# A Chebyshev graph layer's first sweep: the last row's end in two halves of 256 columns, and the other tiles' sums added one tile ahead

## The chip, the core and the metric

The kernel runs on one core of a Trainium2 chip. It uses TensorE (PE, matmuls and transposes into PSUM), VectorE (DVE), ScalarE (ACT), GpSimd (POOL) and the DMA queues of SyncE (SP), ACT and POOL. The metric is the device time of one execution in microseconds (us); the time of a kernel is the median of its runs. The profiles are single executions taken by the hardware profiler, and their times count from the first instruction ("span").

## The reference

Four graph layers run one after the other over the same 4096 x 4096 matrix, each with a residual and a layer norm. The change touches layer 0 and the beginning of layer 3.

```python
# layer 0: x is 4096 x 64, L is adj (4096 x 4096), weight is 4 x 64 x 64
terms = [x, L @ x]
for _ in range(2, K):                       # K = 4
    terms.append(2.0 * (L @ terms[-1]) - terms[-2])
out = jnp.einsum('kni,kio->no', jnp.stack(terms, axis=0), weight)
x = _layernorm(x + out)
...
# layer 3: log map between all pairs of rows, weighted by adj / deg
log_ij = _logmap(x[:, None, :], x[None, :, :], c)
agg = jnp.einsum('ij,ijc->ic', w, log_ij)
x = _layernorm(x + _expmap(origin, agg @ weight + bias, c))
```

## The kernel before

**Layout.** The 4096 rows are 32 blocks of 128; four blocks are a group (8 groups, NG). A tile is 512 rows of group g by 512 columns of chunk c. `cheb_n[:, block, n, :]` holds three terms of 64 features per block: term 0 is ready from the start, term 1 of a group is added to when that group's first sums are done, term 2 after that.

**The first sweep** (the loop `for g in range(NG)`, L643) goes through the rows g = 0 to 7, and in each row through c = 7 down to 0. One pass of the inner loop loads a raw tile (L121, SP queue), turns it block by block on PE (L657), copies it out on ACT (`at`, L664), stores it (L686, POOL queue), and then reduces the raw tile twice on DVE: row sums (`dpart`, L688) and minimum (`lows`, L690). The products of a tile are one tile late: `tile_before`, called behind the next tile's transposes. Tiles with c >= g multiply term 0 only, 64 columns at a time in the two halves of the bank `h_ps` (`halves`, L559); at c = g these sums go to SBUF as `t_h`. Tiles with c < g multiply terms 0 and 1 at once, 128 columns into the bank `w_ps` (`both`, L566). So the lower half of `w_ps` holds more of the first sums, the upper half a part of the second sums.

**The end of a row** is `after_first` (L598), called when the products of c = 0 have been issued. It adds the lower half of `w_ps` to `t_h` (L604, DVE), copies the upper half to `t_w` (L605, ACT), and returns four steps. `first` turns `t_h` on PE and adds it into term 1 (`twice_into`: L580 transposes and two additions for groups above 4, L585 products with `pair`, which add the two halves of a block, and one addition for the others; L588 is the addition). `on_diagonal` multiplies the diagonal tile with the new term 1 into the bank `d_ps` and adds `t_w`, giving `t_d` (L614). `second` does with `t_d` for term 2 what `first` did for term 1, and `taken_off` subtracts term 1 from `nat_a` on POOL (L622). For rows 0 to 6 the steps are taken one per pass of the next row's loop. For row 7 nothing follows, and they run behind the loop, L693 to L695.

**The second sweep** (L745) starts then. Its first product (`pass2`, L566, bank `h_ps`) is that of group 6 with chunk 7, and needs terms 1 and 2 of group 7. Its tiles are loaded on the SP queue (L712) into the buffers that held raw tiles, and each is compared with 0 on DVE (`four`/`mask`, L754). SP also waits for a flag, `no_negative` (L706), which is worked out from `lows` by a one-column product (`low_ps`, L705).

**What sets the order.** Instructions in `in_order(...)` keep their place among each other on their engine; the others may be moved ahead by the scheduler that builds the program, as far as their operands allow. Every engine then works off its own list in order and waits on semaphores.

**Layer 3** is a loop of steps `n`, two for each 512 x 512 tile of pairs, with pieces of several steps interleaved: PE products (`product(n + 2)`, L1494; `opposite`, L1513; `gather`, L1555 and L1567; `turn`, L1539), ACT functions (L1503, L1718, L1719, L1745, L1754) and DVE work (L1521, L1728, L1731, L1743, L1541). At the end of every step one entry of the list `seam` is run (L1757). On entry to the loop the list holds 14 steps: for groups 0 and 1 and then for groups 2 and 3 the end of layer 2 (`ends`: sums, roots, rest, `prepare`, and one `turn_prepared` for each group, L1217 and L1218, which puts the group's features into `tr_a`, also named `tr_c`), and then `weights` and `factors`. `product(12)` and `product(13)` read group 2 in `tr_c`. At one step per `n` the turn of group 2 is run at the end of n = 10.

Of the kernel before, what the change touches and what calls it, by code (L numbers as in the profile page):

```python
# [9 lines left out]
F32 = mybir.dt.float32  # L10
# [5 lines left out]
ALU = mybir.AluOpType  # L16
# [46 lines left out]
def gnn4_kernel(  # L63
# [21 lines left out]
    nc = tc.nc  # L85
    P = 128
    N, F = x.shape
    NB = N // P
    GB = 4
    GW = GB * P  # L90
    NG = NB // GB
    CB = 4
# [49 lines left out]
    pair = const.tile([P, F], F32, name="pair")  # L142
# [25 lines left out]
    nat_a = keep.tile([P, NB, F], F32, name="nat_a")  # L168
# [36 lines left out]
    def in_order(ins):  # L205
        return tc.keep_in_program_order(ins)

    def cols(b):
        return slice(b * P, (b + 1) * P)

    def gblocks(g):
        return slice(g * GB, (g + 1) * GB)
# [312 lines left out]
    with tc.tile_pool(name="acc", bufs=1) as acc_p, tc.tile_pool(  # L525
        name="cols0", bufs=4
    ) as cols_p, tc.tile_pool(name="kept0", bufs=1) as kept_p, tc.tile_pool(name="diag0", bufs=2) as diag_p, tc.tile_pool(
        name="ps_t0", bufs=3, space=PSUM
    ) as ps_t, tc.tile_pool(name="ps_a0", bufs=1, space=PSUM) as ps_a, tc.tile_pool(
        name="ps_p0", bufs=2, space=PSUM  # L530
    ) as ps_p:

        cheb_n = acc_p.tile([P, NB, 3, F], F32, name="cheb_n")

        t_w = [acc_p.tile([P, GW], F32, name=f"t_w{q}") for q in range(2)]
# [28 lines left out]
        def both(ps, k, rhs, jb, first, last):  # L564

            in_order(nc.tensor.matmul(ps, lhsT=cheb_n[:, jb, k : k + 2, :], rhs=rhs, start=first, stop=last))  # L566

        def out_of(ps, name):
            t = acc_p.tile([P, GW], F32, name=name, tag=name if name == "t_h" else "tcol", bufs=2)
            nc.scalar.copy(t, ps)  # L570
            return t

        def new_post(w=F):
            return ps_p.tile([P, GB, w], F32, name="post", tag="post")
# [49 lines left out]
            return [first, on_diagonal, second, taken_off]  # L624


        win = ExitStack()
        win_p = win.enter_context(tc.tile_pool(name="win", bufs=1, side="right"))
        loads, weight_steps = attention_weights(win_p, ps_p)
# [6 lines left out]
        while weight_steps:  # L636
            row, c = divmod(len(aside), NCH)
# [5 lines left out]
        for g in range(NG):  # L643
            h_ps = ps_a.tile([P, GW], F32, name="h_ps")
            w_ps = ps_a.tile([P, GW], F32, name="w_ps") if g else None
            row = {}
            for c in reversed(range(NCH)):
                raw = first_raw.pop() if first_raw else load_raw(g, c)
                if g == NG - 1 and 4 <= c < g:
                    at = kept_p.tile([P, CB, GW], F32, name="at", tag="at") if c == g - 1 else before[:, c - 4]  # L650
                else:
                    at = (diag_p if c == g else cols_p).tile([P, CB, GW], F32, name="at", tag="at")
                for k in range(CB):
                    jb = c * CB + k
                    tp = ps_t.tile([P, GW], F32, name="tp", tag="tp")
                    for b in range(GB):
                        in_order(nc.tensor.transpose(tp[:, cols(b)], raw[:, b, cols(k)], ident))  # L657
                        if g * GB + b == jb:
                            scrap = sm.tile([P, P], F32, name="scrap")
                            in_order(nc.vector.scalar_tensor_tensor(  # L660
                                scrap, raw[:, b, cols(k)], 1.0, ident, ALU.mult, ALU.mult,
                                accum_out=diag[:, jb : jb + 1],
                            ))
                    nc.scalar.copy(at[:, k, :], tp)  # L664
                if steps0:
                    steps0.pop(0)()
                if tile_before:
                    tile_before()

                def tile_before(h_ps=h_ps, w_ps=w_ps, c=c, at=at, g=g, row=row):  # L670
                    for k in range(CB):
                        jb = c * CB + k
                        if c < g:
                            both(w_ps, 0, at[:, k, :], jb, c == g - 1 and k == 0, c == 0 and k == CB - 1)
                        else:
                            halves(h_ps, 0, at[:, k, :], jb, c == NCH - 1 and k < 2, c == g and k >= CB - 2)
                    if c == g:
                        row["at"] = at
                        row["t_h"] = out_of(h_ps, "t_h")
                    if c == 0:  # L680
                        steps0.extend(after_first(g, row["t_h"], w_ps, row["at"]))

                if aside:
                    for work in aside.pop(0):
                        work()
                nc.gpsimd.dma_start(adj_t[g][:, c * CB : (c + 1) * CB, :], at)  # L686

                in_order(nc.vector.tensor_reduce(dpart[:, g, c, :], raw, AX.X, ALU.add))  # L688
                n = g * NCH + c
                in_order(nc.vector.tensor_reduce(lows[:, n : n + 1], raw.rearrange("p b j -> p (b j)"), AX.X, ALU.min))  # L690
                if g == NG - 1 or (g == NG - 2 and c == g):
                    here[g, c] = at
# [52 lines left out]
        for g in reversed(range(NG - 1)):  # L745
            ps = ps_a.tile([P, GW], F32, name="pass2", tag=("h_ps", "w_ps")[g % 2])
            for c in reversed(range(g + 1, NCH)):
                at = load0(g, c)
# [16 lines left out]
        due, n = [], 0  # L765
        for m, g in enumerate(third_rows):
            ps = ps_a.tile([P, GW], F32, name="pass3", tag=("h_ps", "w_ps")[m % 2])
            row = list(reversed(range(g + 1)))
            if m == 0:
                row = row[4:] + row[1:4] + row[:1]  # L770
            for c in row:
                at = load0(g, c, None if (g, c) in here else third_pools.pop(0))
# [399 lines left out]
    for signed in (False, True):  # L1172
        with cmp.Else() if signed else tc.If(all_positive > 0) as block:
            cmp = block
            with tc.tile_pool(name="cols1", bufs=3 if not signed else 2) as cols_p, tc.tile_pool(name="sign1", bufs=1) as sg, tc.tile_pool(
                name="tail1", bufs=1
            ) as tl, tc.tile_pool(name="ps_a1", bufs=1 if signed else 2, space=PSUM) as ps_a, tc.tile_pool(
                name="ps_p1", bufs=2, space=PSUM
# [141 lines left out]
    with tc.tile_pool(name="mask2", bufs=3) as mk_p, tc.tile_pool(name="wt2", bufs=3) as wt_p, tc.tile_pool(  # L1320
        name="ps_c2", bufs=1, space=PSUM
    ) as ps_c, tc.tile_pool(name="ps_a2", bufs=1, space=PSUM) as ps_a, tc.tile_pool(
        name="ps_p2", bufs=2, space=PSUM
# [30 lines left out]
        for turn, groups in enumerate(turns_of):  # L1354
# [9 lines left out]
            for h in reversed(range(2 * NB)):  # L1364
                jb, odd = divmod(h, 2)
                c, k = divmod(jb, CB)
# [59 lines left out]
    with tc.tile_pool(name="o3", bufs=1) as op, tc.tile_pool(name="cols3", bufs=3) as cols_p, tc.tile_pool(  # L1426
# [278 lines left out]
        n = 0  # L1705
        while n < NU + 2 or turns or gathers:
            if n % 2:
                load_own((n + 1) // 2)
                load_mirrored((n - 1) // 2)
            after = gather(*gathers.pop(n)) if n in gathers else []  # L1710
            turned = [w for what in turns.pop(n, []) for w in turn(what)]
            if n < NU:
                if n % 2 == 0:
                    fs[n // 2] = fp.tile([P, CB, GW], F32, name="f3")
                w, cs = ws[n][:, :, columns(n)], columns(n)
                rts[n] = el.tile([P, HB, GW], F32, name="rt3")
                rt = rts[n][:, :, cs]
                nc.scalar.activation(w, w, AF.Ln)  # L1718
                nc.scalar.activation(rt, w, AF.Exp, scale=0.5)  # L1719
                square(n + 1)  # L1720
                opposite(n + 1)
            if n >= 2 and n - 2 < NU:
                m = n - 2
                t, h = divmod(m, 2)
                cm = columns(m)
                hs = slice(h * HB, (h + 1) * HB)
                f, at = fs[t][:, hs, cm], own[t][:, hs, cm]
                nc.vector.scalar_tensor_tensor(  # L1728
                    f, rts.pop(m)[:, :, cm], T_MAX, ws.pop(m)[:, :, cm], ALU.min, ALU.mult
                )  # L1730
                nc.vector.tensor_tensor(at, at, f, ALU.mult)  # L1731
                diagonal = tiles[t][0] == tiles[t][1]
                before = t - 1 if t and tiles[t - 1][0] != tiles[t - 1][1] else None
                gathers[n + 1] = (t, h, before)
                if diagonal and h == 0:
                    late_turns[n + 1] = (t, 0)
                if not diagonal and h == 1:
                    turns.setdefault(n + 1, []).append((t, 0))
                    turns.setdefault(n + 2, []).append((t, 1))
            for work in turned:  # L1740
                work()
            if n < NU:
                nc.vector.scalar_tensor_tensor(rt, vs[n][:, :, cs], (1.0 + V_FLOOR) * SCALE, rt, ALU.max, ALU.add)  # L1743
                product(n + 2)
                nc.scalar.activation(w, w, AF.Exp, scale=-0.5)  # L1745
            late = turn(late_turns.pop(n)) if n in late_turns else []
            for work in after:
                work()
            less_one(n + 1)
            for work in late:  # L1750
                work()
            if 0 < n <= NU:
                rt = rts[n - 1][:, :, columns(n - 1)]
                nc.scalar.activation(rt, rt, AF.Ln, scale=1.0 / SCALE)  # L1754
            if n == NU - 6:
                seam += [ahead_of_last(g) for g in seq[-2:]]
            if seam:  # L1757
                seam.pop(0)(ps_p)
            if n + 6 < NU and tiles[(n + 6) // 2][0] not in rights:
                i = tiles[(n + 6) // 2][0]  # L1760
                rights[i] = right(i)
            n += 1
# [51 lines left out]
```

## Time and profile before

| What | Value |
|---|---|
| Runs | 1411.5, 1417.04 and 1420.06 us, median 1417.04 us |
| Profiled execution, its own time | 1415.59 us |
| Its span | 1413.9 us |
| Mean granted TensorE clock | 0.976 of full speed |
| Busy: PE, DVE, ACT, POOL | 1308.5, 1052.1, 803.7, 109.8 us |
| Last product of the first sweep ends | 351.75 us |
| First product of the second sweep starts | 359.64 us |
| Layer 3's first products start | 976.5 us |

PE is busy for most of the span, but a busy share is an average over stages. For the change the stretch from 340 to 372 us and the beginning of layer 3 (976 to about 1060 us) are of interest. In the rows, L566 is line 566 of the kernel, `t_h<-w_ps,t_h` is what is written from what is read, x4 is a number of instructions, and the brackets say how long the engine had been idle and what released it. A float32 matmul shows as two passes, so four matmuls of 512 columns are x8.

### The profile page before, as it was taken

What the parts mean: (1) busy time and instruction counts of PE and PEld (TensorE: products, weight loads), DVE (VectorE), ACT (ScalarE), POOL (GpSimd) and SP (SyncE); (2) the same over time, 40 slices, a digit from 0 to 9 for tenths busy, and PEclk for the clock granted to TensorE, in tenths of its full rate; (3) what the DMA queues carried; (4) which work ended last, traced back from release to release, by engine and by line L of the source; (5) the groups of instructions that cost most, each with busy time, mean ns of one, the idle gap of its engine ahead of it and who ended that gap; (6) DMA issues with size and microseconds to landing.
All of it is one profiled execution on the core that took longest, in us unless ns stands there. A gap on an engine that the chain in (4) does not pass through costs nothing.

```text
span 1413.9 us, 18980 instructions
## 1 busy us (share of the span) xinstructions
PE 1308.5 (93%) x6766; PEld 604.3 (43%) x6766; DVE 1052.1 (74%) x2012; ACT 803.7 (57%) x1339; POOL 109.8 (8%) x191
## 2 busy tenths in 40 slices
PE   7999999999899998999999999998888899989893
PEld 5655555565344333444444333333333333333331
DVE  6799999898343266788885123446999999999986
ACT  5544443443000115654423675744989999999993
POOL 2110111110122000000110000000000000000000
PEclk9999999999999999999998999998899999999997
DMA  9999999999699999999985555444245454445420
GB/s 326 408 412 411 397 411 409 409 396 398 230 365 388 380 421 378 377 345 331 329 310 191 186 185 179 146 154 175 66 177 189 148 232 150 182 155 202 154 97 12
DMA packets 108191, 382.16 MB, mean 270 GB/s; under 512 B 20276, under 2 KB 20280, under 8 KB 76472
## 3 DMA queue, kind: packets, MB, share of 16 engines
q1 hardware_dynamic: 87096, 296.17, 57.1%
q0 software_dynamic: 12736, 76.29, 13.1%
q10 hardware_dynamic: 8256, 8.39, 1.7%
q8 instruction: 56, 0.92, 0.3%
q14 instruction: 47, 0.39, 0.1%
HBM read 294.05 MB, written 85.20 MB: 268 GB/s over the span
## 4 chain that ended last, share of the span: by engine, by line
PE 59%; ACT 17%; DVE 15%; DMA 4%; issue 3%; ACTq 0%; DVEq 0%; SPq 0%
PE a_ps L1111 8%; PE pass L566 7%; PE w_ps L566 5%; PE tp L657 5%; PE p_ps L1102 5%; PE pass L559 5%; PE cnt_ps L1373 4%; PE acc_ps L1333 4%; DMA raw<-in_adj_dram 3%; ACT w L1718 3%; ACT rt L1719 3%; ACT w L1503 3%; DVE lows L690 2%; ACT rt L1754 2%; DVE dpart L688 2%
## 5 line engine op out<-in xcount | busy, mean ns | idle before, releaser
L664 ACT COPY at<-tp 128x512 f32<-128x512 f32 x248 | 127.8, 598 | 120.8 <-issue 91.1
L1378 ACT ACTIVATE wt<-cnt_ps 128x512 uint16<-128x512 f32 x208 | 115.5, 595 | 72.6 <-PE cnt_ps L1373 67.9
L688 DVE TENSOR_REDUCE dpart<-raw 128x4 f32<-128x2048 f32 x64 | 145.5, 2275 | 5.5 <-DMA raw<-in_adj_dram 5.3
L1555 PE MATMUL sums_ps<-at_d,some 128*64 128x512 f32 x288 | 146.5, 629 | 2.7 <-DVE at_d L1534 1.7
L690 DVE TENSOR_REDUCE lows<-raw 128x1 f32<-128x2048 f32 x64 | 145.5, 2274 | 0.0
L657 PE MATMUL tp<-ident,raw 128*128 128x128 f32 x1024 | 130.8, 281 | 10.1 <-DMA raw<-in_adj_dram 9.0
L657 PEld LDWEIGHTS tp<-ident,raw 128*128 128x128 f32 x1024 | 114.7, 143 | 47.2 <-issue 36.3
L1111 PE MATMUL a_ps<-at,nat_a 128*64 128x512 f32 x512 | 123.3, 609 | 0.0
L1567 PE MATMUL sums_ps<-at_m,some 128*64 128x512 f32 x224 | 110.2, 615 | 0.0
L1494 PE MATMUL v_ps<-rv,tr_a 64*128 64x512 f32 (+1 forms) x288 | 81.7, 645 | 23.2 <-DVE rt L1743 23.2
L566 PE MATMUL pass<-at,cheb_n 128*128 128x512 f32 x224 | 99.2, 601 | 2.4 <-DVE cheb_n L588 1.9
L566 PE MATMUL w_ps<-at,cheb_n 128*128 128x512 f32 x208 | 93.5, 593 | 0.0
L1743 DVE SCALAR_TENSOR_TENSOR rt<-v_ps,rt 128x1024 f32<-128x1024 f32 x72 | 83.5, 1161 | 4.2 <-ACT rt L1719 3.6
L1373 PE MATMUL cnt_ps<-m,follow 128*64 128x512 fp8e4 x480 | 81.7, 391 | 4.6 <-ACT wt L1378 1.5
L1728 DVE SCALAR_TENSOR_TENSOR f<-rt,w 128x1024 f32<-128x1024 f32 x72 | 83.6, 1163 | 1.1 <-ACT rt L1754 1.0
L1731 DVE TENSOR_TENSOR at_d<-at_d,f 128x1024 f32<-128x1024 f32 x72 | 83.7, 1162 | 0.1
L1541 DVE TENSOR_TENSOR at_m<-post,at_m 128x512 f32<-128x512 f32 x112 | 75.4, 686 | 9.5 <-PE post L1539 9.2
L1380 DVE TENSOR_SCALAR wt<-cnt_ps 128x512 uint16<-128x512 f32 x48 | 33.2, 692 | 63.1 <-PE cnt_ps L1373 60.4
L1754 ACT ACTIVATE rt<-rt 128x1024 f32<-128x1024 f32 x72 | 72.1, 1005 | 7.8 <-DVE rt L1743 7.4
L1718 ACT ACTIVATE w<-w 128x1024 f32<-128x1024 f32 x72 | 71.9, 1000 | 5.0 <-DVE w L1521 5.0
L1539 PE MATMUL post<-ident,f 128*128 128x128 f32 x448 | 69.0, 284 | 5.4 <-DVE at_m L1541 4.3
L1745 ACT ACTIVATE w<-w 128x1024 f32<-128x1024 f32 x72 | 72.4, 1006 | 0.6
(396 smaller groups left out, 2222.7 us busy)
## 6 DMA issues: line engine op xcount, KB each, us to landing
at<-adj_t SPq DMA_DIRECT2D x119, 1024.0 KB, 7.9
raw<-in_adj_dram SPq DMA_DIRECT2D x64, 1024.0 KB, 13.5
adj_t<-at POOLq DMA_DIRECT2D x62, 1024.0 KB, 8.1
at_d<-adj_t SPq DMA_DIRECT2D x36, 1024.0 KB, 4.8
at_m<-adj_t SPq DMA_DIRECT2D x28, 1024.0 KB, 6.9
m<-mask_t SPq DMA_DIRECT2D x120, 128.0 KB, 2.8
m<-mask_t SPq DMA_DIRECT2D x60, 256.0 KB, 4.1
mask_t<-mask ACTq DMA_DIRECT2D x28, 256.0 KB, 7.9
```

Source lines behind the costliest of these rows:

```text
L566: in_order(nc.tensor.matmul(ps, lhsT=cheb_n[:, jb, k : k + 2, :], rhs=rhs, start=first, stop=last))
L657: in_order(nc.tensor.transpose(tp[:, cols(b)], raw[:, b, cols(k)], ident))
L664: nc.scalar.copy(at[:, k, :], tp)
L688: in_order(nc.vector.tensor_reduce(dpart[:, g, c, :], raw, AX.X, ALU.add))
L690: in_order(nc.vector.tensor_reduce(lows[:, n : n + 1], raw.rearrange("p b j -> p (b j)"), AX.X, ALU.min))
L1111: in_order(nc.tensor.matmul(ps[q * F : (q + 1) * F, :], lhsT=nat_a[:, c * CB + k, 0:F], rhs=of[q if signed else 0][:, k, :], start=(c == 0 ...
L1373: in_order(nc.tensor.matmul(cnt[a][r * HP : (r + 1) * HP, :], lhsT=follow, rhs=chunks[c][odd][2 * a + r][:, k, :], start=(h == 2 * NB - 1) ...
L1378: in_order(nc.scalar.activation(wt[odd][a], cnt[a], AF.Relu, scale=-128.0))
L1555: in_order(nc.tensor.matmul(bank[0:F, :], lhsT=nat_c[:, j * CB + k, :], rhs=own[t][:, k, :], start=(i == j and k == 0), stop=(j == seq[-1] ...
L1567: in_order(nc.tensor.matmul(bank[F:P, :], lhsT=nat_c[:, above * GB + k, :], rhs=mirrored[tm][:, k, :], start=(k == 0 and above == seq[0]), ...
L1718: nc.scalar.activation(w, w, AF.Ln)
L1754: nc.scalar.activation(rt, rt, AF.Ln, scale=1.0 / SCALE)
```

## The change

There are three parts. Row 7's end is a function of its own, `end_of_last`, called in place of the products of c = 0: these are done in two halves of 256 columns, the first in the bank `h_ps` and the second in `w_ps`, and everything behind them (the additions, the diagonal products in `d_ps` and `h_ps`, the additions into terms 1 and 2) goes half by half in an order written out by hand. The turns for row 7 are products with `pair`, two blocks at a time, so that one addition is enough. In row 7, the sums of the other tiles (c = 6 to 1) are closed with c = 1 (the last flag of `both`) and added to `t_h`, and copied to `t_w`, right behind the products of c = 1: `before_last`. In layer 3, two entries of `seam` are run at n = 0, so that every entry of the first list comes one step earlier.

```diff
+        def before_last(g, t_h, w_ps):
+            in_order(nc.vector.tensor_tensor(t_h[0:F, :], w_ps[0:F, :], t_h[0:F, :], ALU.add))
+            nc.scalar.copy(t_w[g % 2][F:P, :], w_ps[F:P, :])
+
+        def end_of_last(g, t_h, diag_at, at):
+
+            HW = GW // 2
+            two = [slice(0, HW), slice(HW, GW)]
+            gs, t_w7 = gblocks(g), t_w[g % 2]
+            t_d = acc_p.tile([P, GW], F32, name="t_d", tag="tcol", bufs=2)
+            pairs, w_two, d_two = {}, {}, {}
+
+            def last_products(h, ks):
+                if h not in w_two:
+                    w_two[h] = ps_a.tile([P, GW], F32, name=("h_ps", "w_ps")[h])
+                for k in ks:
+                    in_order(nc.tensor.matmul(
+                        w_two[h][:, 0:HW], lhsT=cheb_n[:, k, 0:2, :], rhs=at[:, k, two[h]], start=(k == 0), stop=(k == CB - 1)
+                    ))
+
+            def add_last(h):
+                cs, w = two[h], w_two[h]
+                in_order(nc.vector.tensor_tensor(t_h[0:F, cs], w[0:F, 0:HW], t_h[0:F, cs], ALU.add))
+                in_order(nc.vector.tensor_tensor(t_w7[F:P, cs], w[F:P, 0:HW], t_w7[F:P, cs], ALU.add))
+
+            def paired(t, h):
+                pairs[h] = o = new_post()
+                for b in range(2):
+                    in_order(nc.tensor.matmul(o[:, b, :], lhsT=t[:, cols(2 * h + b)], rhs=pair, start=True, stop=True))
+
+            def twice_half(n, h):
+                to = cheb_n[:, g * GB + 2 * h : g * GB + 2 * h + 2, n, :]
+                in_order(nc.vector.scalar_tensor_tensor(to, pairs[h][:, 0:2, :], 2.0, to, ALU.mult, ALU.add))
+
+            def diagonal(h, ks):
+                if h not in d_two:
+                    d_two[h] = ps_a.tile([P, GW], F32, name=("d_ps", "h_ps")[h])
+                for k in ks:
+                    q = k % 2
+                    in_order(nc.tensor.matmul(
+                        d_two[h][q * F : (q + 1) * F, 0:HW], lhsT=cheb_n[:, g * GB + k, 1, :], rhs=diag_at[:, k, two[h]],
+                        start=(k < 2), stop=(k >= 2), skip_group_check=True,
+                    ))
+
+            def add_diagonal(h):
+                in_order(nc.vector.tensor_tensor(t_d[:, two[h]], d_two[h][:, 0:HW], t_w7[:, two[h]], ALU.add))
+
+            last_products(0, range(CB))
+            add_last(0)
+            last_products(1, (0, 1))
+            paired(t_h, 0)
+            twice_half(1, 0)
+            last_products(1, (2, 3))
+            add_last(1)
+            for h in range(2):
+                diagonal(h, (0, 1))
+            paired(t_h, 1)
+            twice_half(1, 1)
+            for h in range(2):
+                diagonal(h, (2, 3))
+                add_diagonal(h)
+            for h in range(2):
+                paired(t_d, h)
+                twice_half(2, h)
+            nc.gpsimd.tensor_tensor(nat_a[:, gs, :], nat_a[:, gs, :], cheb_n[:, gs, 1, :], ALU.subtract)
...
                 def tile_before(h_ps=h_ps, w_ps=w_ps, c=c, at=at, g=g, row=row):
+                    if g == NG - 1 and c == 0:
+                        end_of_last(g, row["t_h"], row["at"], at)
+                        return
                     for k in range(CB):
                         jb = c * CB + k
                         if c < g:
-                            both(w_ps, 0, at[:, k, :], jb, c == g - 1 and k == 0, c == 0 and k == CB - 1)
+                            both(w_ps, 0, at[:, k, :], jb, c == g - 1 and k == 0, c == (g == NG - 1) and k == CB - 1)
...
                     if c == g:
                         row["at"] = at
                         row["t_h"] = out_of(h_ps, "t_h")
+                    if g == NG - 1 and c == 1:
+                        before_last(g, row["t_h"], w_ps)
                     if c == 0:
                         steps0.extend(after_first(g, row["t_h"], w_ps, row["at"]))
...
-            if seam:
-                seam.pop(0)(ps_p)
+            for _ in range(2 if n == 0 else 1):
+                if seam:
+                    seam.pop(0)(ps_p)
```

## The prediction, made before the changed kernel ran

> **What bounds the kernel now.** I read the page first, for which engine fills the span and which engine the last-ending chain runs over.
>
> ```profile
> PE 1308.5 (93%) x6766; PEld 604.3 (43%) x6766; DVE 1052.1 (74%) x2012; ACT 803.7 (57%) x1339; POOL 109.8 (8%) x191
> PE 59%; ACT 17%; DVE 15%; DMA 4%; issue 3%; ACTq 0%; DVEq 0%; SPq 0%
> ```
>
> The kernel is a sequence of stages, most of them bound by TensorE (PE); averages say little about one edit. The change touches two places: the seam between the first and the second sweep of layer 0, and the first 14 steps of layer 3's loop. So next comes the chain of waits around the first seam (columns: start in us, length, what).
>
> ```profile
> 344.87 6.88 PE w_ps L566 x16
> ...
> 351.78 0.69 DVE t_h L604
> ...
> 354.15 1.96 PE d_ps L559 x8
> ...
> 358.12 1.13 DVE four L754
> ...
> 359.64 8.83 PE pass L566 x16
> ```
>
> PE ends the first sweep's products at 351.75 (344.87 + 6.88) and starts the second sweep at 359.64: a seam of 7.89 us, in which DVE and PE take turns, about 0.04 us at each hand-over, and in which a mask compare of 1.13 us (L754) happens to stand between the two last additions. Also, 16 passes take 8.83 us behind the seam and 6.88 ahead of it, so another 1.95 us goes to a slower PE. The windows of 1 us (columns: window, length, busy time and number of each engine, then PEclk, DMA share, GB/s) show why.
>
> ```profile
> 358.00:359.00 1.00, 0.00 (x0) 0.00 (x0) 1.00 (x3) 0.00 (x0) 0.00 (x0) 1.00 0.00 0
> 359.00:360.00 1.00, 0.36 (x1) 0.36 (x2) 0.59 (x2) 0.00 (x0) 0.13 (x1) 0.89 0.00 0
> 360.00:361.00 1.00, 1.00 (x2) 0.37 (x2) 0.00 (x0) 0.00 (x0) 0.44 (x1) 0.50 0.00 0
> 363.00:364.00 1.00, 1.00 (x3) 0.42 (x2) 0.00 (x0) 0.00 (x0) 0.00 (x0) 0.90 0.00 0
> ```
>
> The granted clock is 0.50 from about 359.8 to 363.2. Last, the timeline of the seam, for what DVE does before its first addition.
>
> ```profile
> 343.67 2.27 DVE L688 TENSOR_REDUCE dpart<-raw 128x4 f32<-128x2048 f32 x1
> ...
> 345.86 2.27 DVE L690 TENSOR_REDUCE lows<-raw 128x1 f32<-128x2048 f32 x1
> ...
> 351.78 0.68 DVE L604 TENSOR_TENSOR t_h<-w_ps,t_h 64x512 f32<-64x512 f32 x1 [2.76 <-PE w_ps L566]
> ```
>
> The two reduces over the last tile's raw rows (c = 0) end at 348.1, beside PE's products. They cost nothing now.
>
> **The change part by part.** *Where the early addition stands.* The products of tile c = 1 end at 344.87 + 3.44 = 348.31. The addition of these sums to t_h (before_last) is issued inside the loop's pass for c = 0, ahead of that pass's two reduces, and all three are kept in program order. The order of DVE's queue in the built program says the same: reduces of c = 1, addition, reduces of c = 0, additions of the first half. So DVE, free at 343.7, waits for PE until 348.31, adds (0.69, to 349.03), and only then runs the two reduces, 2.19 each by the chain's rows: to 353.4. Queued behind them is all of end_of_last's DVE work. The cover of 4.4 us that the reduces had is gone, and they lie on the path.
>
> *The new tail, step by step.* PE multiplies the first half of c = 0 from 348.31: half of 3.44, to 350.03. Then two of the second half's four (a quarter of 3.44, to 350.9), and then waits 3 us. DVE adds the first half at 353.4; 512 columns take 0.69, 256 elements 0.42, so to 353.83. The pair product of two blocks is half of the x8 row of L585 (1.00 in the timeline): with the hand-over to 354.40. The addition into cheb_n, 128 elements, 0.28 by rows of that shape: 354.71. PE does the other two products meanwhile, 354.40 to 355.26. DVE has six small instructions queued here, which the scheduler put there (they ran with a seventh from 348.05 to 349.02): to 355.5; then the second half's t_h, to 355.92. Diagonal, first two blocks of both halves: half of d_ps's 1.94 = 0.97, to 356.23; pair product to 356.75, addition to 357.06; the other diagonal products to 358.07; t_d of half 0 at 358.05, half 1 at 358.54; pair products to 358.60 and 359.12; addition of half 0 at 358.93. The low_ps product behind them needs the bank that this addition frees, and takes some 0.15. The second sweep's first products need blocks 0 and 1 alone, and start at 359.2; the last addition (359.4) lies beside them. The compare L754 comes after the additions in the new order. Start against start: 359.64 to 359.2, 0.4 us gained. Of the 8 us seam, the halves and the dropped compare win 4.8 us and the reduces take 4.4 back.
>
> *The slower clock.* Count busy PE time in stretches of 3.4 us, the length of the slow one: 356.4 to 359.8 held 28% and was followed by 0.50, 353.0 to 356.4 held 62% and was not. With the change, if the stretches lie alike, 349.6 to 353.0 holds 1.3 of 3.4 us (38%), the next 70%, the next 90%. Four outcomes: no slow stretch, 0.4 + 1.95 = 2.4 us gained; one at the start of the second sweep as now, 0.4; one in the middle of the tail, where pair, products and diagonal on the path take about 1.3 more but the sweep starts at full clock, 0.4 + 1.95 - 1.3 = 1.1; both, 0.9 lost. 38% is nearest the row of 28%, so one slow stretch is likeliest: between 0.4 and 1.1, and I take 1.0 of a gain.
> The Trainium skill (TensorE: Matmul & The Clock Gate, Part 1) lets the clock fall after an idle window of about 3.4 us. The new seam's longest idle stretch, 2.97 us, is shorter, so by that rule no slow stretch comes and the gain is 2.4 us. In this trace the longest fully idle stretch of the old seam was 1.92 us and the clock fell all the same, so a mostly idle window is enough, and I go by the rows.
>
> *What rides along.* The fifth load of the second sweep waits for the last reduce on SP's queue: issued at 353.4 instead of 348.1, landing some 8.9 us later (median of the loads here), at 362; its tile is used at 376.8, so 14 us of cover. The load behind it waits on SP for no_negative (358.1, now about 359.6), but also for the first tile's buffer, which the second sweep itself frees later. The copy to t_w (ACT, 0.58) and the subtraction on POOL (0.73) are beside other work; if the reduces did not hide the copy, it would cost 0.58.
>
> *Two seam steps at n = 0 of layer 3.* The same instructions come one step of the loop earlier until n = 13; from n = 14 on the list is empty in both, and the issue order is the same again. DVE is nearly full there:
>
> ```profile
> 1020.00:1030.00 10.00, 8.51 (x42) 3.08 (x41) 10.00 (x16) 9.25 (x11) 0.00 (x0) 1.00 0.53 196
> 1050.00:1060.00 10.00, 7.84 (x44) 3.95 (x44) 9.71 (x17) 9.86 (x12) 0.00 (x0) 1.00 0.55 211
> ```
>
> From 980 to 1090, DVE is busy 105.8 of 110 us, and its work there is unchanged. So the most that a better order wins is its 4.2 us of idle time. The loss: one pair of instructions turns round.
>
> ```profile
> 1040.73 1.13 PE L1494 MATMUL v_ps<-rv,tr_a 64*128 64x512 f32 x4
> ...
> 1043.59 0.42 DVE L1218 COPY tr_a<-post 128x256 f32<-128x256 f32 x1
> ```
>
> Product 12 reads the place of group 2 in tr_a and the copy waits for it; with the step at n = 9, the product waits for the copy, and the opposite products, squares and everything after wait for that product. The copy is queued on DVE between rt of n = 9 and rt of n = 10, and product 12 needs rt of n = 10 to free its bank anyway: no added wait. If it came late it would cost up to one step, 5.2 us (rt at 1019.63 and 1024.83). Between -4.2 and +5.2 I take 0, since a full DVE with equal work is what the rows show.
>
> *Sum.* 1.0 off the profiled execution's 1415.59: 1414.6. That execution lies 1.45 below the median of the runs, 1417.04; for the median I forecast 1416.0. PE runs without gaps through the rest of the second sweep, so what the seam wins isn't given back there.
>
> **Rivals.** *The seam wins what halving can win.* If the reduces were not ahead of the first half's addition, it would come right behind the products (350.07), the rest of the tail would be shorter by 3.3 us, and with the small instructions out of the way the second sweep starts near 355.6: 4 us, with a warm clock up to 6. About 5 off: median 1412. For it: PE's numbers. Against it: DVE's queue order.
> *Slower: layer 3's product waits.* Place: product 12. Price: up to one step of 5.2 us, less the 1.0 won: median 1417.0 + 4.2 = 1421.2. It decides once the copy lands over 1.0 us after rt of n = 10. For it: transposes, copy and product are now a chain across PE, DVE and PE in an engine pair that is 85 to 100% busy. Against it: the queue positions.
> *Nothing moves:* two slow stretches (0.9 lost) and a neutral layer 3, or the gain lost in a later wait for a load: median 1417 to 1418. For it: 38% of a stretch is no clear case. Against it: only one slow stretch follows a seam of equal length now.
>
> **How the numbers follow.** Forecast 0.55, full gain 0.12, layer 3's wait 0.15, nothing 0.18. All lie within 6 us of 1417, that is 0.4%. A measurement of this kernel can tell about 1% (14 us) from no change; the three runs shown spread from 1411.5 to 1420.06. To pass 1% an effect would have to be twice the whole seam: faster 0.03, within 1% 0.94, slower 0.03. The range takes in the full gain with 2 us of scatter below, and the wait in layer 3: 1409.5 to 1421.5.
>
> **What would show it.** Right: in the trace after, DVE idle from the reduce of c = 1 to about 348.3, then an addition, both reduces, and the first 64x256 addition near 353.4; PE idle about 3 us between; first pass of the second sweep near 359; at most one stretch of clock 0.50 around the seam. In layer 3 the same 5.2 us steps and no idle PE ahead of product 12. Wrong: the first half's addition near 350 (then the full gain), or a PE wait on tr_a's copy in layer 3.

## The result, and the profile after

The changed kernel is slower. Its median is 1419.64 us (20 runs, 1414.61 to 1423.13), against 1414.86 us for the kernel before in the same comparison (20 runs). The ratio is 1.0031, interval 1.0019 to 1.0043, so the loss is 2.7 to 6.1 us and 4.4 us in the middle. The profiled execution has a span of 1420.0 us at a mean clock of 0.974. Lines of the new `before_last`, `end_of_last` and layer 3 are 71 lines lower than in the kernel before.

The page of the changed kernel, busy time and the chain's shares by engine:

```profile
PE 1315.5 (93%) x6790; PEld 610.7 (43%) x6790; DVE 1054.6 (74%) x2017; ACT 803.1 (57%) x1339; POOL 111.3 (8%) x191
PE 60%; ACT 17%; DVE 13%; DMA 6%; issue 3%; ACTq 0%; DVEq 0%; SPq 0%
```

PE is busy 7.0 us longer than before (1315.5 against 1308.5), with hardly more rows (6790 against 6766): its products took longer. The chain of waits around the seam (start in us, length, what) says where:

```profile
344.09 3.45 PE w_ps L566 x8
...
347.63 0.68 DVE t_h L628
...
350.43 2.27 DVE lows L761
352.70 0.34 DVE t_h L649
...
353.09 1.11 PE post L655 x4
354.20 1.81 PE w_ps L643 x4
...
361.33 1.90 PE post L655 x8
...
363.35 8.40 PE pass L566 x16
```

The products of c = 1 end at 347.54, the reduces stand on the path (`lows`), and the first half is added at 352.6. DVE had been idle for 4.68 us ahead of the early addition (timeline; the bracket gives the idle time and what ended it):

```profile
347.63 0.68 DVE L628 TENSOR_TENSOR t_h<-w_ps,t_h 64x512 f32<-64x512 f32 x1 [4.68 <-PE w_ps L566]
```

PE is idle from 350.12 until the first pair products at 353.09, for 2.97 us. Then four pair products take 1.11 us and two products of 256 columns 1.81. The second sweep starts at 363.35. From the end of c = 1's products to the end of the sweep's first 16 passes the changed kernel needs 15.81 + 8.40 = 24.21 us; before it was 11.33 + 8.83 = 20.16. So this execution loses 4.05 us at the seam. The windows of 1 us (window, length, busy time and number of PE, PEld, DVE, ACT, POOL, then PEclk, DMA share, GB/s) show how:

```profile
350.00:351.00 1.00, 0.12 (x1) 0.00 (x0) 1.00 (x2) 0.00 (x0) 0.00 (x0) 1.00 0.97 410
351.00:352.00 1.00, 0.00 (x0) 0.00 (x0) 1.00 (x1) 0.00 (x0) 0.00 (x0) 1.00 1.01 426
352.00:353.00 1.00, 0.00 (x0) 0.00 (x0) 1.00 (x2) 0.00 (x0) 0.00 (x0) 0.68 0.51 213
...
354.00:355.00 1.00, 1.00 (x4) 0.82 (x5) 0.76 (x7) 0.00 (x0) 0.00 (x0) 0.50 0.71 254
...
358.00:359.00 1.00, 0.97 (x4) 0.78 (x4) 0.00 (x0) 0.00 (x0) 0.00 (x0) 0.50 0.00 0
359.00:360.00 1.00, 0.65 (x4) 0.46 (x6) 0.29 (x1) 0.00 (x0) 0.62 (x1) 0.50 0.00 0
...
362.00:363.00 1.00, 1.00 (x6) 1.00 (x5) 0.29 (x1) 0.00 (x0) 0.00 (x0) 0.50 0.00 0
...
366.00:367.00 1.00, 1.00 (x4) 0.52 (x3) 0.00 (x0) 0.00 (x0) 0.00 (x0) 0.99 0.52 197
367.00:368.00 1.00, 1.00 (x4) 0.44 (x3) 0.00 (x0) 0.00 (x0) 0.00 (x0) 1.00 0.18 66
```

PE stands still from 350.12 on, and from about 352.4 to 366.0 the clock is 0.50: 13.65 us, four times the 3.4 us of one stretch. In these four stretches PE is busy for 2.68, 3.20, 3.25 and 3.42 us, so the whole hand-written tail ran at half speed.

In layer 3, the idle times of DVE (timeline between 1030 and 1060; the brackets give the idle time and what ended it) are these two, where the kernel before had only 0.20 and 0.15 us:

```profile
1048.69 1.23 DVE L1814 SCALAR_TENSOR_TENSOR rt<-v_ps,rt 128x1024 f32<-128x1024 f32 x1 [1.29 <-ACT rt L1790]
...
1058.48 1.42 DVE L1612 TENSOR_TENSOR at_m<-post,at_m 128x512 f32<-128x512 f32 x2 [2.00 <-PE post L1610]
```

Counted from each kernel's own step 0, the addition `rt` of step 16 is 1.97 us late and that of the loop's last step 2.71 us.

### The profile page after: what moved, and what is told of

The parts are those of the page before. It is cut to its first block, busy times and chain, and to the rows that moved or that the text cites. A ratio compares the mean times of both kernels' runs of the same rounds, so it can differ in the third digit from the quotient of the medians.

```text
span 1420.0 us, 19033 instructions
## 1 busy us (share of the span) xinstructions
PE 1315.5 (93%) x6790; PEld 610.7 (43%) x6790; DVE 1054.6 (74%) x2017; ACT 803.1 (57%) x1339; POOL 111.3 (8%) x191
## 4 chain that ended last, share of the span: by engine, by line
PE 60%; ACT 17%; DVE 13%; DMA 6%; issue 3%; ACTq 0%; DVEq 0%; SPq 0%
PE a_ps L1182 8%; PE pass L566 7%; PE tp L723 6%; DMA raw<-in_adj_dram 5%; PE w_ps L566 5%; PE p_ps L1173 5%; PE pass L559 5%; PE cnt_ps L1444 4%; PE acc_ps L1404 4%; PE h_ps L559 3%; ACT w L1789 3%; ACT rt L1790 3%; ACT w L1574 2%; ACT rt L1825 2%; ACT wt L1449 2%
## 5 line engine op out<-in xcount | busy, mean ns | idle before, releaser
L566 PE MATMUL w_ps<-at,cheb_n 128*128 128x512 f32 x200 | 90.1, 593 | 0.0
```

## The experiments

The trace after points at two places. Theory A: the loss sits at the seam, where the reduces stand on the path and PE's wait for them slows its clock. Theory C: the second seam step costs time in layer 3. The expectations of each run give what these and their rivals say of it; the theories W, G and B of the later runs are formed where they come up. All ratios are to the kernel before, with their intervals; "seam" is the time from the end of c = 1's products to the second sweep's start.

**Reduces first.** The changed kernel with the early sum behind the reduces.

```diff
-                    if g == NG - 1 and c == 1:
-                        before_last(g, row["t_h"], w_ps)
...
                 in_order(nc.vector.tensor_reduce(lows[:, n : n + 1], raw.rearrange("p b j -> p (b j)"), AX.X, ALU.min))
+                if g == NG - 1 and c == 0:
+                    before_last(g, row["t_h"], w_ps)
```

> The changed kernel with one call moved: the early addition of the other tiles' sums is issued behind the two reduces of the tile c = 0 and not ahead of them. I measure the seam from the end of the products of c = 1 to the first product of the second sweep: 11.33 us in the kernel before (348.31 to 359.64), 15.81 us in the changed one (347.54 to 363.35). Theory A (the reduces stand on the path, and PE, idle meanwhile, goes on at half clock): the 4.4 us of reduces run beside the products again, the seam falls to 7.5 to 9.5 us depending on whether a slow stretch falls into it, and the time to 1411 to 1415. Theory B (the halves cost by themselves, by more and shorter products and more hand-overs): the seam stays above 11.3 us and the time at 1417 or more.

Measured: 1412.67 us, ratio 0.9978 (0.9966 to 0.9991). Its chain around the seam:

```profile
346.51 3.44 PE w_ps L566 x8
349.94 1.73 PE h_ps L643 x8
351.67 1.09 PE w_ps L643 x4
352.76 0.39 PE post L655 x4
...
357.24 1.10 PE post L655 x8
...
358.47 7.07 PE pass L566 x16
```

The seam is 8.5 us, PE hardly waits, no stretch of half clock follows, and the 16 passes take 7.07 us. Layer 3 is as late as in the changed kernel (1.94 us at step 16). Moving one addition behind two reduces turned a loss into a gain: theory A holds, and theory B of this expectation (the halves cost by themselves) falls. How much of it is the reduces and how much the clock, the next run tells.

**Warm wait.** The changed kernel, with three unread products in the place where PE waits; the reduces stay on the path.

```diff
             last_products(1, (0, 1))
+            warm = ps_t.tile([P, GW], F32, name="tp", tag="tp")
+            for k in range(3):
+                in_order(nc.tensor.matmul(warm, lhsT=cheb_n[:, k, 0:2, :], rhs=at[:, k, :], start=(k == 0), stop=(k == 2)))
             paired(t_h, 0)
```

> The changed kernel with three products of 512 columns more, into a bank that nobody reads, in PE's wait for the reduces (2.97 us idle; the three take 2.6 us at full clock). Theory A, the clock's part: the stretch of 13.65 us at clock 0.50 that begins in this wait does not begin there, the tail's products run at full clock, the seam falls from 15.8 to about 11 us and the time by 3 to 5, to about 1415.5. If the clock is a by-product and DVE's additions and hand-overs set the pace, the seam stays within 1 us of 15.8.

Measured: 1415.44 us, ratio 1.0003 (0.9992 to 1.0013), that is 4 us less than the changed kernel by doing more. Its chain:

```profile
352.55 0.34 DVE t_h L649
...
352.94 0.66 PE post L655 x4
353.60 0.92 PE w_ps L643 x4
...
358.91 7.06 PE pass L566 x16
```

The first half is added as late as in the changed kernel (5.16 us behind c = 1's products in both chains), but the four pair products take 0.66 us instead of 1.11, the two half products 0.92 instead of 1.81, the 16 passes 7.06, and the clock is 1.00 throughout. So the reduces by themselves cost 3 us of seam (11.5 against 8.5), and the wait that they make for PE cost up to 5.6 more through the clock (24.21 against 18.58) in these profiles.

**One seam step.** The changed kernel with the old single step in layer 3.

```diff
-            for _ in range(2 if n == 0 else 1):
-                if seam:
-                    seam.pop(0)(ps_p)
+            if seam:
+                seam.pop(0)(ps_p)
```

> The changed kernel with one seam step at n = 0 of layer 3, as before; the first sweep's end is as changed. In the profiles, 1.95 us of the change's loss came between steps 0 and 16 of layer 3, 3.3 us ahead of it. Theory C (the earlier order in layer 3 costs about 2 us): step 16 of layer 3 starts 1.5 to 2 us earlier after step 0 than in the changed kernel (92.81 us), at 90.9, and the time is 1417.6. Rival D (the 1.95 us are where the slow stretches of the clock happen to fall): the median stays within 1 us of 1419.6.

Measured: 1414.95 us, ratio 1.0005 (0.9989 to 1.0022); step 16 of layer 3 is 0.52 us earlier than before, so 2.5 us earlier than in the changed kernel. Rival D's time (within 1 us of 1419.6) falls; that the 2 us of layer 3 depend on the clock comes up again below. The median fell by more than 2.5 us, by 3.7 us by the ratios, but each of the two ratios is uncertain by some 2 us, so this does not tell 3.7 from 2.5. Its seam, whose code is that of the changed kernel, was 13.16 us with one stretch of half clock in place of four, and 20.23 us to the end of the 16 passes. The same instructions thus cost 20.2 or 24.2 us, as the clock falls. In this profile PE's wait of 2.97 us lies inside one stretch (354.4 to 357.8, PE busy for 0.61 us); the slow stretch behind it, 357.8 to 361.2, is full of PE work, and the clock is 1.00 again. In the changed kernel's profile the clock falls inside the wait, and the first slow stretch is not full.

**Two seam steps alone**, in the kernel before.

> The kernel before with only the last part of the change: two seam steps at n = 0 of layer 3. Theory C: slower by 2 us, 1417. Rival D: within 1 us of 1414.9. The seam between the sweeps stays at 11.3 us in both.

Measured: 1419.46 us, ratio 1.0028 (1.0016 to 1.0040): 4.0 us lost by the ratio (5.1 by the two medians), more than the 2 expected; steps 2.06 us late at step 16 and 2.51 at the loop's end. Its first seam, which is unchanged code, took 12.69 us, not the expected 11.3: it met a longer slow stretch than the kernel before showed (windows of 2 us):

```profile
356.00:358.00 2.00, 2.00 (x8) 0.59 (x8) 0.00 (x0) 0.00 (x0) 0.72 (x1) 0.72 0.72 303
...
360.00:362.00 2.00, 0.94 (x6) 0.51 (x4) 1.14 (x3) 0.00 (x0) 0.00 (x0) 0.50 0.02 4
...
364.00:366.00 2.00, 2.00 (x4) 0.89 (x3) 0.00 (x0) 0.00 (x0) 0.00 (x0) 0.50 0.35 131
```

Three stretches here, one in the kernel before. Over six profiles of the old seam, time to the end of the 16 passes was 20.0 to 21.9 us. So single profiles of a seam differ by 2 us in the old code and 4 in the new, and the median over many runs has to decide.

**Both losses out.** Reduces first, and one seam step.

> The changed kernel with both of its presumed losses taken out: the early sum stands behind the two reduces of the last tile, and layer 3 takes one seam step at n = 0 as before. If the two losses are separate (theory), this is the kernel with the reduces first (1412.7) less the 4.7 to 5.1 us that the second seam step cost in the two runs about it: 1407.6 to 1408.0, ratio to the kernel before about 0.995; seam of about 8.5 us, no stretch of clock 0.50 at it, layer 3's step 16 within 0.6 us of the kernel before. Rival: the clock's slow stretches only move elsewhere, and the parts do not add: 1411 to 1413.

Measured: 1409.87 us, ratio 0.9965 (0.9954 to 0.9976): 4.9 us faster than the kernel before, the best version of all; seam 8.53 us, no slow stretch at it, step 16 of layer 3 0.50 us early. The time lies between the theory's and the rival's: ratio by ratio, the second seam step cost 1.8 us here, 3.7 in the changed kernel and 4.0 in the kernel before. Each of these is uncertain by 2 to 3 us, so they do not contradict one common cost of about 3.

**Which of the fourteen steps?** Four more edits of the kernel before move part of the list. First, all but the weights and factors:

```diff
-        seam += [weights, factors]
+        seam += [lambda ps_p: None, weights, factors]
...
+            for _ in range(2 if n == 0 else 1):
```

> The kernel before with two seam steps at n = 0 and an empty step ahead of the weights' step: twelve steps come one step earlier, weights and factors stay at n = 12 and 13. Theory W (the loss in layer 3 is the weights' step at n = 11: its transposed rows wait on VectorE behind two long instructions, TensorE waits 1.8 us for them, and VectorE then waits for TensorE): within 1.5 us of the kernel before, VectorE idle under 0.6 us between 1040 and 1062. Rival G (the twelve steps of the two groups cost): 4 to 5 us slower, as with all fourteen steps moved (+5.1).

Then only these two (the second step taken at n = 11):

> The kernel before with the second seam step taken at n = 11 instead of n = 0: only the weights' step (n = 11) and the factors' (n = 12) come one step earlier, the twelve steps ahead of them stay. Theory W: TensorE idle about 1.8 us ahead of the product of the weights (line 1600, one line later here), VectorE idle over 1 us between 1046 and 1062, 2 to 5 us slower than the kernel before. Rival G: as the kernel before, within 1.5 us.

Measured: ratio 1.0018 (1.0006 to 1.0031) and steps 3.22 us late at step 16 for the first; 1.0009 (0.9996 to 1.0023) and 0.06 us for the second. The first has neither what theory W foresaw (within 1.5 us, DVE idle under 0.6) nor what rival G did (4 to 5 us): it lost 2.5 us by the ratio, between the two. In the second, the wait that theory W named is there, but DVE is idle for only 0.61 us between 1046 and 1062 (theory W: over 1), and what the wait delays is made up again by step 16:

```profile
1054.29 0.43 PE L1600 MATMUL post<-wh,spread_t 64*128 64x64 f32 x2 [1.58 <-DVE spread_t L1598]
```

So that wait by itself costs nothing in this profile, whose clock is 1.00 there; its median leaves 0.6 us of gain to 3.3 of loss. In the first (timeline), PE idles ahead of the transposes of group 2, and DVE later behind PE:

```profile
1034.58 0.69 PE L1217 MATMUL post<-ident,some 128*128 128x128 f32 x2 [2.26 <-DVE at_m L1541]
...
1039.23 1.88 PE L1494 MATMUL v_ps<-rv,tr_a 64*128 64x512 f32 x4
...
1042.05 1.09 PE L1539 MATMUL post<-ident,f 128*128 128x128 f32 x8
...
1042.74 1.29 DVE L1541 TENSOR_TENSOR at_m<-post,at_m 128x512 f32<-128x512 f32 x2 [2.15 <-PE post L1539]
```

There are two `post` banks. Group 2's transposes take one of them as soon as `at_m` has freed it, so the mirrored transposes (L1539) come behind the sums and the product, and DVE waits 2.15 us for them. Two edits test this. Only the two transposing steps early:

```diff
+        seam += [lambda ps_p: None, weights, factors]
...
+            for _ in range(2 if n == 9 else 1):
```

> The kernel before with the second seam step taken at n = 9 and an empty step ahead of the weights' step: of the fourteen steps only the two of turn_prepared for the last two groups (steps 10 and 11 of the list) come one step earlier. Theory B (these transposes now come right behind the mirrored transposes, which hold both banks of the tag post until VectorE has multiplied, so TensorE stands still about 2.3 us and the next products are late): TensorE idle about 2.3 us ahead of the transposes at line 1217, layer 3's steps 2.5 to 3.5 us late from step 16 on, median 2 to 4 us above the kernel before. Rival: the earlier steps (sums, roots, rest of the layer norms) do it: steps and median as before, within 1 us and 1.5 us.

And the ten steps ahead of them early, the transposes where they were:

```diff
+        seam[10:10] = [lambda ps_p: None]
         seam += [weights, factors]
...
+            for _ in range(2 if n == 0 else 1):
```

> The kernel before with two seam steps at n = 0 and an empty step ahead of the last two groups' turn_prepared: the ten steps ahead of it come one step earlier, the two transposing steps, weights and factors stay. Theory B: no idle stretch over 1.2 us ahead of the transposes at line 1217, layer 3's steps from 16 on within 0.7 us of the kernel before, median within 1.5 us. Rival: the ten steps cost 2.5 to 3.5 us.

The first lost most, ratio 1.0035 (1.0021 to 1.0049), 5.57 us late at step 16, but not by the wait foreseen. Its inputs were not moved with it, and PE waited for them:

```profile
1039.25 0.66 PE L1217 MATMUL post<-ident,some 128*128 128x128 f32 x2 [3.39 <-DVE some L1203]
```

So it proves nothing for the bank. The other is the clean comparison. With the half clock from 1034.4 to 1041.2 (1034.0 to 1040.8 with the transposes early, practically the same place) its mirrored transposes stand ahead of the product:

```profile
1035.13 1.97 PE L1539 MATMUL post<-ident,f 128*128 128x128 f32 x8 [2.26 <-DVE at_m L1541]
1037.03 2.08 PE L1494 MATMUL v_ps<-rv,tr_a 64*128 64x512 f32 x4
```

DVE's idle time behind PE is gone, and step 16 is 0.69 us late instead of 3.22. The wait of 2.26 us for the bank is there all the same, so in this pair of profiles it was not the wait of PE that cost, as theory B had it, but what was queued behind it at half clock. The medians do not show it: the ratio is 1.0015 (1.0004 to 1.0026), against 1.0018 with the transposes early, although the loop's last step was 0.18 us early in the profile. Its profiled seam met two stretches of half clock, which gives part of that and no more.

**Layer 3 and the clock.** The order at the `post` banks is not what made the changed kernel late. There (first two rows) and with the reduces first (next three) DVE's wait of 2.00 us stands behind the weights' step, the place of theory W: PE is idle for the transposed rows (`spread_t`), the clock is 0.50 from 1052.1 to 1058.9 (1045.8 to 1052.6), and the mirrored transposes take 1.85 and 1.84 us, where the kernel before needs 1.09. The last three rows are the warm-wait kernel, whose layer 3 is the same code but whose clock happened to be 1.00 from 995 to 1175:

```profile
1053.10 0.69 PE L1671 MATMUL post<-wh,spread_t 64*128 64x64 f32 x2 [1.77 <-DVE spread_t L1669]
1057.32 1.85 PE L1610 MATMUL post<-ident,f 128*128 128x128 f32 x8
...
1046.80 0.69 PE L1671 MATMUL post<-wh,spread_t 64*128 64x64 f32 x2 [1.76 <-DVE spread_t L1669]
1051.02 1.84 PE L1610 MATMUL post<-ident,f 128*128 128x128 f32 x8
1052.18 1.42 DVE L1612 TENSOR_TENSOR at_m<-post,at_m 128x512 f32<-128x512 f32 x2 [2.00 <-PE post L1610]
...
1042.77 1.23 DVE L1817 SCALAR_TENSOR_TENSOR rt<-v_ps,rt 128x1024 f32<-128x1024 f32 x1 [1.30 <-ACT rt L1793]
1047.17 0.43 PE L1674 MATMUL post<-wh,spread_t 64*128 64x64 f32 x2 [1.76 <-DVE spread_t L1672]
1049.40 1.09 PE L1613 MATMUL post<-ident,f 128*128 128x128 f32 x8
```

At full clock PE's wait of 1.76 us and DVE's of 1.30 us for ACT are there as well, but DVE waits nowhere for PE, and step 16 is 0.29 us early. Counted from step 0, the additions `rt` of the three kernels agree within 0.02 us up to step 12; from step 13 on the warm-wait kernel is 2.23 and 2.26 us ahead of the other two. So in these profiles the new order costs layer 3 nothing at full clock, and the 2 us are the price of the half clock behind PE's new wait. Unread products in the waits of layer 3 were not tried.

**All runs side by side.** "Seam and 16 passes" is the time from the end of c = 1's products to the end of the second sweep's first 16 passes in the profiled execution, "half clock" the slow time met there, "step 16" how late layer 3's step 16 is against the kernel before, counted from step 0.

| Kernel | Ratio to before | Seam and 16 passes, us | Half clock, us | Step 16, us |
|---|---|---|---|---|
| before | 1 | 20.16 | 3.4 | 0 |
| changed | 1.0031 | 24.21 | 13.65 | +1.97 |
| reduces first | 0.9978 | 15.59 | none | +1.94 |
| warm wait | 1.0003 | 18.58 | none | -0.29 |
| one seam step | 1.0005 | 20.23 | 3.4 | -0.52 |
| reduces first, one step | 0.9965 | 15.59 | none | -0.50 |
| before, two steps | 1.0028 | 21.93 | 10.2 | +2.06 |
| before, two steps, weights kept | 1.0018 | 20.16 | 3.4 | +3.22 |
| before, weights early | 1.0009 | 21.94 | 10.2 | +0.06 |
| before, transposes early | 1.0035 | 20.01 | 3.4 | +5.57 |
| before, ten steps early | 1.0015 | 21.57 | 6.8 | +0.69 |

The mean granted clock is on record for every run, not for the profiled ones alone. In the traces it is either 1.00 or 0.50, so twice the missing share of the span is the time at half clock, an estimate. It is about 66 us a run in the changed kernel (mean clock 0.9768 over 20 runs) and 56 us in the kernel before (0.9802 over the 35 runs beside the first four experiments); 65 us with two seam steps alone, 60 with the warm wait, 57 each with the reduces first and with one seam step; and 50 with the reduces first and one step, against 58 in the kernel before beside it. Each is uncertain by 1 to 3 us. So it is not only the profiled execution in which the changed kernel spends more time at half clock: about 10 us more of it go with the 4.4 us lost.

## Why the prediction was wrong, step by step

**Right: the queue.** The first half was to be added 5.09 us behind the end of c = 1's products (353.4 less 348.31); it was added 5.09 us behind (352.63 in the timeline less 347.54). DVE idles 4.68 us, adds, and reduces twice, as the order of its queue said. PE's wait of 3 us was foreseen as well.

**Nearly right: the tail at full clock.** From there to the second sweep the prediction had 5.8 us; the warm-wait kernel, with the same tail at clock 1.00, took 6.36. The sum of rows was 0.6 us short.

**The step that failed first: "one slow stretch is likeliest".** It counted PE's busy share in stretches of 3.4 us, found 38%, 70% and 90%, and took the nearest row of the old seam. The shares were nearly right (1.17 of 3.41 us ahead of the fall, then 79%, 94% and 95%); what it read from them was not. Its worst outcome was two stretches and 0.9 us lost. The profiled execution had four, with PE busy for most of it, and lost 4.05 us; another execution of the same seam had one and lost 0.07, where the forecast for one stretch was 0.4 to 1.1 us of gain (the sum of rows was short, and the stretch cost 1.6 us, 13.16 less 11.52, where 1.3 were reckoned). Two errors lie in the step: that a stretch with PE busy again ends the slow clock (the old seam's row of 62% was one at full clock, and says nothing of the way back), and that only the sweep and one stretch of the tail could be hit. Nearly the whole tail is a chain through PE, so every microsecond of half clock in it counts. What the idle wait starts is priced by what is queued behind it. The Trainium skill (TensorE: Matmul & The Clock Gate, Part 1) lets the clock fall after an idle window of about 3.4 us and return after one busy window. Here an idle time of 2.97 us, and a stretch with PE busy for 1.17 of 3.41 us, was enough, and stretches with 3.20 and 3.25 us of PE work did not bring it back.

**The step that failed next: "Between -4.2 and +5.2 I take 0".** Layer 3's early steps cost 2.0 us by step 16, and by the ratios 3.7 us (with the changed seam) and 4.0 us (alone). "A full DVE with equal work" had no slack to win but much to lose: from 1030 to 1060, its 0.35 us of waiting became 3.29. The prediction looked for the wait at product 12, on group 2's copy, and rightly found none. The term that it put at nothing is another: the new order makes PE wait elsewhere (2.26 us for a `post` bank, 1.77 us for the weights' transposed rows), and the half clock that followed the second of these waits made DVE wait 2.00 us. The prediction priced the clock at the seam only. At full clock the same order cost nothing by step 16 (-0.29 us in the warm-wait kernel's profile). Its bound of one step, 5.2 us, held.

**The sum.** Foreseen 1.0 us of gain; measured 4.4 of loss. Taking the second seam step out gives back 3.7 of it (1.0031 to 1.0005) and leaves 0.7 for the seam, with an interval that reaches from 1.6 of gain to 3.1 of loss; filling PE's wait gives back 4.0 (1.0031 to 1.0003). The two together exceed the loss, in part because the seam at full clock is a gain (18.58 against 20.16 us to the end of the 16 passes); no run has both, and the rest is within the intervals.

**The rivals.** "The seam wins what halving can win" had the arithmetic of the halves right: it put the second sweep 7.3 us behind c = 1's products and the gain at 4 to 6 us if the reduces were not ahead. With the reduces first it was 8.5, the time to the end of the 16 passes fell by 4.6 (20.16 to 15.59), and without layer 3's part the kernel gained 4.9 us. "Layer 3's product waits" had the price (4.2 us slower) but not the place.

**What stays open.** Of the runs that were not profiled only the mean clock is known, not where it fell: how often the seam meets one, two or four stretches, and how often a slow stretch follows PE's new waits in layer 3, stays open. So does why the ten early steps without the transposes still cost 0.6 to 3.7 us in the median.

## What to carry to other kernels

An early partial result is early only if the engine that adds it has nothing else to do first: find what is queued behind the new wait, and if independent work stands there (here two reduces), put the new instruction behind it. A wait of 3 us of TensorE ahead of a serial chain of small products is to be priced with that whole chain at half clock; filling the wait with unread products, or removing it, was worth more here than shortening the chain. When steps of a list are moved by one place, look for the waits that the move makes on TensorE and for what stands in the queue behind them, not only at the data that the steps hand over: those waits can cost nothing at full clock and 2 us at half clock.

## What the runs showed of the hardware

The granted clock fell to 0.50 in multiples of 3.41 us (3.4, 6.8, 10.2, 13.65), at places that differ between executions of the same instructions. With the wait filled, the same narrow products (64 columns wide in `pair`, 256 in the halves) ran at clock 1.00 to the end; once the clock had fallen, it stayed at 0.50 through stretches of 3.41 us with 2.68, 3.20 and 3.25 us of PE work, and was 1.00 again behind one with 3.42. In the kernel before with ten steps early, a slow stretch with 2.99 us of PE work (355.1 to 358.5) was followed by full clock. So busy time alone does not decide when the clock returns. What does decide it, these runs do not show.
